# PSUM banks for short-lived results by a ledger of the plan, and an earlier read of the accumulated y

## The chip, the cores and the metric

The kernel runs on one core of one Trainium2 chip. The metric is the device time of one execution in microseconds; before the change it is 1008.92 us, the median of 3 runs (1008.82 to 1009.45). A core has engines that work side by side, each through its own queue in order: TensorE for matrix products (PE in the profile, its weight loads PEld), VectorE (DVE), ScalarE (ACT), GpSimd (POOL), and SyncE (SP), which here issues transfers. TensorE writes its products into PSUM, which has eight banks of 128 partitions x 512 fp32 values; the results of a bank must be read by VectorE or ScalarE before the bank can be written anew.

## The reference, cut to what matters

The input x is 8 sequences of 1024 tokens with 128 values each, all in fp32. Three layers follow one another:

```python
x = x + 0.5 * ffn(layernorm(x))
x = x + attention(layernorm(x))      # causal, one head of 128, rotary positions
x = x + 0.5 * ffn(layernorm(x))      # the same weights
```

`ffn` is a mixture of 16 experts of width 64. A sigmoid of `x @ gate_w.T` scores the experts; of the scores plus a bias the best four are chosen; their scores, divided by their sum and times 2.5, are the weights. Each expert computes `silu(x @ w1.T) * (x @ w3.T)`, then `@ w2.T`; a shared expert with the weight 1 is added. The kernel computes all 16 experts for every token, with the weight 0 for those not chosen.

## The kernel before

**Groups and periods.** The work of the two ffn layers is cut into 32 groups of 512 tokens (4 tiles of 128; 8 sequences x 2 groups x 2 layers). Each group has one period p, 0 to 31. The order is layer one of sequences 0 to 3, then alternately the second ffn layer of a sequence and the first of a later one, and at last the second of sequences 4 to 7. A period has two phases of eight steps. In the first, step k computes 128 hidden units (two experts) for 512 tokens: `gate(k)` (L265) and the product of `up(k)` (L278), on ScalarE the SiLU (L280), on VectorE the product of the two (L282), on GpSimd the weighting with the expert weights (`weigh`, L286). In the second phase, step k adds the product of those units with the down matrix to y (`down`, L291), which accumulates in one PSUM bank. `close` (L302) then adds y and the shared expert's result on VectorE into yT in SBUF; a period later `add` turns yT back (L324) and adds it to x (L327).

**Slots.** All else goes into slots between these steps: U0 to U8 around the first phase and D0 to D8 in the second; slot Uk+1 follows step k, and slot Dk follows `down(k)`, so that D8 stands alone at the end, after `close`. A plan written out by hand gives each piece its slot. Of the pieces, these matter here:

- `turn` of a group (L168): transposes of the normalised x, copied by ScalarE (L169). The routing: `route_a` (L193, copied by L198), `route_b` (L202), `score` (L207 on ScalarE), then `top_a`, `top_b`, `top_c` on VectorE (L211 to L239, the last writes comb), then `spread`: a transpose of comb (L248), a copy (L250) and the transfers that bring the weights to all partitions (cd, cb). In the steady part these have the slots D4, D5, D7, D7, D8, D8, U1 and U3.
- Attention: `Heads` project q, k and v of a sequence (L394, read by L398, L399 and L400; L408, copied by L412). A `Query` is one tile of 128 queries: `scores` (L427), mask, maximum, exponent (L438), two `turn`s (transposes L454, copied by ScalarE L458 or VectorE L460) and `attend` (L466), whose result VectorE adds to x in L470 and follows with the statistics L145 and L146. A tile i attends to i + 1 tiles, so its attend can be narrow (2 passes) or wide (16). A period starts two or three queries; their attends are in D7, in U2 of the next period and, with a third, in U5.
- `Shared`: the shared expert for a pair of groups, in U0 and U2 of even periods (L342, L346, L347, L356, L362).

The Tile framework puts in the waits between engines; nothing is reordered after that.

**PSUM banks.** Bank 0 takes the up product of even k, then y; bank 1 the gate of even k; 2 and 3 those of odd k. Queries use 4 and 5 or 2 and 3 for scores, projections and the shared expert use 5 and 4. All other results, those of `turn`, `route_a`, `route_b`, `spread`, `add`, `values` and `attend`, are short-lived: written by a few matmuls and read by one or two instructions. They ask `other_bank()` (L74), which goes round through a list of spare banks: 6 and 7, and bank 1 as well from D0 to D7. There are 353 such takes.

Of the kernel before, what the change touches and what calls it, by code (L numbers as in the profile page):

```python
# [26 lines left out]
def kernel(  # L27
# [24 lines left out]
    NP = EI // P  # L52
# [10 lines left out]
    dram = ctx.enter_context(tc.tile_pool(name="dram", bufs=3, space=bass.MemoryType.DRAM))  # L63
    ps_all = ctx.enter_context(tc.tile_pool(name="ps_all", bufs=1, space=PSUM))

    psum = ps_all.tile([P, 8 * W], F32, name="psum")

    def bank(i, n=1):
        return psum[:, i * W : (i + n) * W]


    spare = [6, 7]

    def other_bank():  # L74
        spare.append(spare.pop(0))
        return bank(spare[-1])

    def tiles_of(ap):
        return ap.rearrange("p (j q) -> p j q", q=P)
# [59 lines left out]
    def stats(key, b, tiles):  # L139

        if key not in mvs:
            mvs[key] = small.tile([P, NT, 2], F32, tag="mv", name=f"mv_{key}", bufs=16)
        for t in tiles:
            st = small.tile([P, 6], F32, tag="st", name=f"st_{key}_{t}")
            nc.vector.bn_stats(st, xs[b][:, t, :])  # L145
            nc.vector.bn_aggr(mvs[key][:, t, :], st)  # L146
# [18 lines left out]
    def transposed(key, g, xn, hT):  # L165
        pt = other_bank()
        for j in range(GT):
            nc.tensor.transpose(tiles_of(pt)[:, j, :], xn[:, j, :], ident)  # L168
        nc.scalar.copy(hT, pt)  # L169
# [3 lines left out]
    class Group:  # L173
# [15 lines left out]
        def route_a(self):  # L189

            lt = other_bank()[:, :P]
            for j in range(GT):
                nc.tensor.matmul(  # L193
                    lt[j * SW : (j + 1) * SW, :], gw, self.hT[:, j * P : (j + 1) * P],
                    start=True, stop=True, tile_position=(0, j * SW),
                )
            self.lt = small.tile([P, P], F32, tag="lt", name=f"lt_{self.nm}", bufs=2)
            nc.scalar.copy(self.lt, lt)  # L198

        def route_b(self):  # L200
            self.lg = other_bank()[:, :P]
            nc.tensor.transpose(self.lg, self.lt, ident)  # L202
# [279 lines left out]
    NPER = NG * len(order)  # L482
# [7 lines left out]
    def at(p, slot, *fs):  # L490
        jobs.setdefault((p, slot), []).extend(fs)
# [3 lines left out]
    def when(p, slot):  # L495
        return p * len(slots) + slots.index(slot)

    turn_of = {(gr.layer, gr.b, gr.g): p for p, gr in enumerate(groups)}


# [2 lines left out]
    for p in range(3, 29):  # L503
        for n in range(2 if p in (15, 21) or (p % 2 == 0 and p != 26) else 3):
            if not queue:
                continue
            b, i = queue.pop(0)
            starts.setdefault(b, p)
            q = Query(heads[b], i)
            s, first, e, t0, t1, a = (  # L510
                ((p, "U7"), 4, (p, "D0"), (p, "D3"), (p, "D5"), (p, "D7")),
                ((p, "D2"), 2, (p, "D5"), (p, "D8"), (p + 1, "U0"), (p + 1, "U2")),
                ((p, "D4"), 4, (p, "D7"), (p + 1, "U3"), (p + 1, "U4"), (p + 1, "U5")),
            )[n]
            at(*s, lambda q=q, first=first: q.scores(first))
            at(*e, q.exp)
            at(*t0, lambda q=q: q.turn(0))
            at(*t1, lambda q=q: q.turn(1))
            at(*a, q.attend)
            done[b, i] = when(*a)  # L520
# [4 lines left out]
    for b in range(B):  # L525
        h, st = heads[b], starts[b]
        ready = when(turn_of[0, b, 1] + 1, "U7")
        if b == 0:
            p0, p1 = st - 1, st - 1
            places = ("U8", "D0", "D2", "D3", "D5", "D6", "D7", "D8")  # L530
        else:
            p0, p1 = st - 2, st - 1
            places = ("D0", "D3", "D5", "D8", "U1", "U4", "U5", "U6")
        assert ready < when(p0, places[0])
        at(p0, places[0], h.deviations)
        at(p0, places[1], lambda h=h: h.norm(0))
        at(p0, places[2], lambda h=h: h.norm(1))
        at(p0, places[3], lambda h=h: h.turn(0))
        at(p1, places[4], lambda h=h: h.turn(1))
        at(p1, places[5], lambda h=h: h.project(0, 0))  # L540
        at(p1, places[6], lambda h=h: h.project(1, 0))
        at(p1, places[7], lambda h=h: h.values(0))
        at(st, "U4", lambda h=h: h.project(0, 1))
        at(st, "U5", lambda h=h: h.project(1, 1))
        at(st, "U6", lambda h=h: h.values(1))


    for p, gr in enumerate(groups):
        steps = (
            gr.norm_a, gr.norm_b, gr.turn, gr.route_a, gr.route_b, gr.score, gr.top_a, gr.top_b,  # L550
            gr.top_c, gr.spread,
        )
        if p == 1:
            steps = steps[1:]
            places = [(0, s) for s in ("U3", "U5", "U6", "U8", "D0", "D1", "D2", "D3", "D6")]
        else:
            places = [(p - 2, s) for s in ("U5", "D1", "D4", "D5", "D7", "D7", "D8", "D8")]
            places += [(p - 1, "U1"), (p - 1, "U3")]
        if p > 0:
            for f, place in zip(steps, places):  # L560
                at(*place, f)
        if gr.layer == 1:
            for t in range(gr.g * GT, (gr.g + 1) * GT):
                assert done[gr.b, t] < when(p - 2, "U5")

        if p % 2 == 0:
            pair = Shared(groups[p : p + 2])
            if p == 0:
                at(0, "D0", pair.up)
                at(0, "D3", pair.down)  # L570
            else:
                jobs[p, "U0"] = [pair.up] + jobs.get((p, "U0"), [])
                at(p, "U2", pair.down)

        at(p + 1, "U3", gr.add)
        if gr.layer == 0:
            t = gr.g * GT
            for s in ("U5", "U7"):
                at(p + 1, s, lambda b=gr.b, t=t: stats(f"a{b}", b, (t, t + 1)))
                t += 2  # L580


    for b in range(2, B):
        p = turn_of[0, b, 0]
# [11 lines left out]
        nc.sync.dma_start(out=cs, in_=rope)  # L596

    def run(p, slot):
        for f in jobs.pop((p, slot), []):
            f()  # L600

# [18 lines left out]
    for p, gr in enumerate(groups):  # L620
        run(p, "U0")
        for k in range(NP):
            gr.up(k)
            if p == 0 and k < 2:
                run(p, f"U{k + 1}")
                if k == 1:
                    gr.weigh(k)
            else:
                gr.weigh(k)
                run(p, f"U{k + 1}")  # L630
        for k in range(NP + 1):
            if k < NP:
                gr.down(k)
            else:
                gr.close()
            if k == 0:
                spare.insert(0, 1)
            elif k == NP:
                spare.remove(1)
            run(p, f"D{k}")  # L640
    for p in (NPER, NPER + 1):
        for slot in slots:
# [73 lines left out]
```

## Time and profile before

| | |
|---|---|
| median of 3 runs | 1008.92 us (1008.82 to 1009.45) |
| the profiled execution | 1008.44 us, span 1006.7 us |
| TensorE matmuls | 985.8 us busy, 98% of the span |
| VectorE / ScalarE / GpSimd | 67% / 44% / 45% busy |
| mean granted TensorE clock | 0.999 of full |
| L265, L278, L291, 512 passes of 128x512 each | 264.0, 262.3, 247.1 us |
| transfers | 80.26 MB, 80 GB/s |

The span is the time from the first to the last instruction of the program in one profiled execution; the time of that execution has something around it. A row of the profile names line, engine, operation, what is written <- what is read, the shape and the count; where it ends in brackets, the engine sat idle that long before it, and what follows the arrow ended the wait. An fp32 product is two passes of a weight load and a matmul each, a transpose one. Matmuls are pipelined: the next starts before the one before has its end in the profile.

### The profile page before, as it was taken

Reading aid. Unit: us, or ns where it says so; the run is one execution under the profiler, and the core shown is the slowest. Engines: PE = TensorE matmul, PEld = TensorE weight load, DVE = VectorE, ACT = ScalarE, POOL = GpSimd, SP = SyncE. Lnnn points to the kernel's source line nnn. Section 1 sums busy time; section 2 is a strip of 40 time slices with the busy share of each in tenths; the row PEclk is TensorE's granted clock in tenths of the full one; section 3 lists DMA queues with packets and bytes.
Section 4 is the critical chain, followed back from the end, with each engine's and each line's share of the span. In section 5 each row is a group of like instructions: output and inputs, shape, how many; then the busy total and the mean of one; then the engine's idle time right before and its main releaser. Section 6 shows DMA issues by size and latency. Waiting matters only on the chain.

```text
span 1006.7 us, 11656 instructions
## 1 busy us (share of the span) xinstructions
PE 985.8 (98%) x3654; PEld 515.9 (51%) x3654; DVE 670.5 (67%) x2035; ACT 444.2 (44%) x798; POOL 450.7 (45%) x379
## 2 busy tenths in 40 slices
PE   8999999999999999999999999999999999999998
PEld 5444455554555555455554555555555555455543
DVE  6776777668666676666768656776667756664553
ACT  3444535444544444343544444544444444443331
POOL 2455556154633464334625455234644454423444
PEclk9999999999999999999999999999999999999999
DMA  6654343043312542145303453034421333134440
GB/s 164 164 122 91 86 85 86 1 105 85 86 41 55 117 85 60 27 96 116 86 15 71 95 117 76 12 83 96 96 59 37 75 96 85 36 72 96 96 95 21
DMA packets 56910, 80.26 MB, mean 80 GB/s; under 512 B 3600, under 2 KB 23440, under 8 KB 56720
## 3 DMA queue, kind: packets, MB, share of 16 engines
q1 hardware_dynamic: 55568, 78.26, 34.5%
q10 hardware_dynamic: 1280, 1.26, 0.4%
q8 instruction: 28, 0.46, 0.2%
q14 instruction: 34, 0.28, 0.1%
HBM read 74.27 MB, written 5.24 MB: 79 GB/s over the span
## 4 chain that ended last, share of the span: by engine, by line
PE 91%; DVE 5%; ACT 1%; POOL 1%; DMA 1%; issue 1%; SPq 0%; DVEq 0%; POOLq 0%
PE psum L291 21%; PE psum L265 20%; PE psum L278 20%; PE psum L466 6%; PE psum L427 6%; PE psum L454 3%; PE psum L342 3%; PE psum L394 3%; PE psum L168 2%; PE psum L356 2%; PE psum L408 1%; PE psum L193 1%; PE psum L324 1%; DVE x L470 1%; DMA cb<-cd 1%
## 5 line engine op out<-in xcount | busy, mean ns | idle before, releaser
L286 POOL TENSOR_TENSOR hidT<-hidT,cb 128x512 f32<-128x512 f32 x256 | 323.2, 1270 | 516.3 <-DVE hidT L282 479.2
L265 PE MATMUL psum<-hT,wg 128*128 128x512 f32 x512 | 264.0, 597 | 0.9 <-DVE x L470 0.5
L278 PE MATMUL psum<-hT,wu 128*128 128x512 f32 x512 | 262.3, 594 | 1.2 <-DVE yT L302 1.2
L291 PE MATMUL psum<-hidT,wd 128*128 128x512 f32 x512 | 247.1, 599 | 0.0
L282 DVE TENSOR_TENSOR hidT<-psum,sg 128x512 f32<-128x512 f32 x256 | 175.4, 687 | 104.0 <-PE psum L278 97.7
L280 ACT ACTIVATE sg<-psum 128x512 f32<-128x512 f32 x256 | 152.4, 598 | 203.7 <-PE psum L265 191.8
L278 PEld LDWEIGHTS psum<-hT,wu 128*128 128x128 f32 x512 | 96.5, 190 | 126.1 <-issue 98.8
L291 PEld LDWEIGHTS psum<-hidT,wd 128*128 128x128 f32 x512 | 89.8, 190 | 80.4 <-issue 74.2
L265 PEld LDWEIGHTS psum<-hT,wg 128*128 128x128 f32 x512 | 88.4, 192 | 68.4 <-issue 61.4
L466 PEld LDWEIGHTS psum<-v,prT 128*128 128x128 f32 x576 | 74.4, 192 | 30.6 <-issue 28.7
L466 PE MATMUL psum<-v,prT 128*128 128x128 f32 x576 | 74.6, 275 | 0.0
L458 ACT COPY prT<-psum 128x512 f32<-128x512 f32 (+2 forms) x64 | 32.4, 506 | 93.9 <-PE psum L454 93.8
L427 PE MATMUL psum<-k,q 128*128 128x512 f32 (+2 forms) x192 | 72.4, 486 | 0.0
L159 DVE TENSOR_SCALAR xn_f<-x,mv_f,rs_f 128x128 f32<-128x128 f32 x128 | 68.5, 595 | 1.9 <-POOL rs_f L152 1.7
L470 DVE SCALAR_TENSOR_TENSOR x<-psum,rl,x 128x128 f32<-128x128 f32 x64 | 22.1, 346 | 69.4 <-PE psum L202 44.8
L427 PEld LDWEIGHTS psum<-k,q 128*128 128x128 f32 x192 | 36.5, 190 | 45.9 <-issue 44.7
L454 PEld LDWEIGHTS psum<-ident,pr 128*128 128x128 f32 x288 | 35.4, 141 | 39.6 <-issue 29.6
L454 PE MATMUL psum<-ident,pr 128*128 128x128 f32 x288 | 47.4, 276 | 5.7 <-DVE x L470 5.2
L433 DVE TENSOR_REDUCE top<-psum 128x1 f32<-128x128 f32 (+3 forms) x64 | 48.5, 758 | 2.2
L438 ACT ACTIVATE pr<-psum,top 128x128 f32<-128x128 f32 (+3 forms) x64 | 47.7, 746 | 0.3
L431 DVE TENSOR_TENSOR psum<-psum,causal 128x128 f32<-128x128 f32 x64 | 19.0, 297 | 41.3 <-PE psum L427 40.8
L152 POOL TENSOR_TENSOR rs_f<-rs_f,neg_half 128x4 f32<-128x4 f32 x32 | 32.4, 1013 | 16.8 <-DVE rs_f L151 16.3
(86 smaller groups left out, 1010.9 us busy)
## 6 DMA issues: line engine op xcount, KB each, us to landing
cb<-cd SPq DMA_DIRECT2D x124, 512.0 KB, 8.2
x<-in_x SPq DMA_DIRECT2D x16, 256.0 KB, 10.3
out_x<-x SPq DMA_DIRECT2D x15, 256.0 KB, 2.4
cb<-cd SPq DMA_DIRECT2D x8, 256.0 KB, 5.8
cd<-cT SPq DMA_DIRECT2D x32, 32.0 KB, 1.8
cs<-in_rope SPq DMA_DIRECT2D x1, 1024.0 KB, 9.7
wg<-in_w_gate ACTq DMA_DIRECT2D x2, 256.0 KB, 6.4
wu<-in_w_up ACTq DMA_DIRECT2D x2, 256.0 KB, 6.0
```

The lines of the kernel that those rows point to most:

```text
L159: nc.vector.tensor_scalar(xn[:, j, :], xs[b][:, t, :], mvs[key][:, t, 0:1], rstd[:, j : j + 1], ALU.subtract, ALU.mult,)
L265: nc.tensor.matmul(bank(2 * (k % 2) + 1), wg[:, units], self.hT, start=True, stop=True)
L278: nc.tensor.matmul(u_ps, wu[:, units], self.hT, start=True, stop=True)
L280: nc.scalar.activation(sg, g_ps, AF.Silu)
L282: nc.vector.tensor_tensor(hid, u_ps, sg, ALU.mult)
L286: nc.gpsimd.tensor_tensor(hid, hid, self.cb[:, k, :], ALU.mult)
L291: nc.tensor.matmul(self.y, wd[:, k, :], self.hidT[:, k, :], start=(k == 0), stop=(k == NP - 1))
L427: nc.tensor.matmul(s[:, c:e], h.q[:, i * P : width], h.k[:, c:e], start=True, stop=True)
L433: nc.vector.tensor_reduce(top, s[:, :width], AX.X, ALU.max)
L438: nc.scalar.activation(self.pr[:, : self.width], self.s[:, : self.width], AF.Exp, bias=self.top, scale=SCALE, accum_out=self.h.rl[:, self. ...
L454: nc.tensor.transpose(tp[:, j, :], self.pr[:, (k + j) * P : (k + j + 1) * P], ident)
L466: nc.tensor.matmul(o, self.prT[:, j, :], self.h.v[:, j, :], start=(j == 0), stop=(j == i))
```

## The change

`other_bank()` no longer goes round through a list. A table `held` notes for each bank the slots in which the plan uses it for something of its own (the calls of `hold`). A bank 1 to 5 is free in a slot if it is held neither in it nor in the one before or after; 6 and 7 are always free. Of the free ones, the bank whose last take is the oldest is given. The lists that put bank 1 in and out at D0 and D8 go away. The projections in `Heads` are put into the plan by a loop at the same slots as before; only the ledger is told of them. And `close` is called right behind `down(7)`, ahead of the pieces of slot D7, where it came after them before.

```diff
-    spare = [6, 7]
+    held = {n: set() for n in range(8)}
+    by_age = [6, 7, 1, 2, 3, 4, 5]
+    now = [-1]
 
     def other_bank():
-        spare.append(spare.pop(0))
-        return bank(spare[-1])
+        for n in by_age:
+            free = not held[n] & {now[0] - 1, now[0], now[0] + 1} and now[0] >= 0
+            if n > 5 or free:
+                by_age.remove(n)
+                by_age.append(n)
+                return bank(n)
...
+    def hold(banks, first, last):
+        for n in banks:
+            held[n] |= set(range(when(*first), when(*last) + 1))
+
+    for p in range(NPER):
+        hold((0,), (p, "U1"), (p, "D8"))
+        hold((1,), (p, "U1"), (p, "U8"))
+        hold((2, 3), (p, "U1"), (p, "D1"))
...
             at(*s, lambda q=q, first=first: q.scores(first))
+            hold((first, first + 1), s, e)
...
-        at(p1, places[5], lambda h=h: h.project(0, 0))
-        at(p1, places[6], lambda h=h: h.project(1, 0))
+        for w in range(2):
+            for p, slot, g in ((p1, places[5 + w], 0), (st, ("U4", "U5")[w], 1)):
+                at(p, slot, lambda h=h, w=w, g=g: h.project(w, g))
+                hold((5 - w,), (p, slot), (p, slot))
         at(p1, places[7], lambda h=h: h.values(0))
-        at(st, "U4", lambda h=h: h.project(0, 1))
-        at(st, "U5", lambda h=h: h.project(1, 1))
...
                 at(0, "D3", pair.down)
+                hold((4, 5), (0, "D0"), (0, "D4"))
...
                 at(p, "U2", pair.down)
+                hold((4, 5), (p, "U0"), (p, "U3"))
...
     def run(p, slot):
+        now[0] = when(p, slot)
...
             if k < NP:
                 gr.down(k)
-            else:
+            if k == NP - 1:
                 gr.close()
-            if k == 0:
-                spare.insert(0, 1)
-            elif k == NP:
-                spare.remove(1)
             run(p, f"D{k}")
```

## The prediction

> **What bounds the kernel now.** I read the busy shares first, then the chain that ended last, then the list of waits, and last the order of time around the waits on TensorE's path.
>
> ```profile
> PE 985.8 (98%) x3654; PEld 515.9 (51%) x3654; DVE 670.5 (67%) x2035; ACT 444.2 (44%) x798; POOL 450.7 (45%) x379
> ...
> PE 91%; DVE 5%; ACT 1%; POOL 1%; DMA 1%; issue 1%; SPq 0%; DVEq 0%; POOLq 0%
> ```
>
> TensorE sets the time: 91% of the chain. VectorE's 5% is what TensorE waits for, so the question is how many waits of TensorE the change takes away. The waits of TensorE's matmuls, as total, times, longest:
>
> ```profile
> PE psum L454 <- DVE x L470: 5.2, 13, 0.4
> PE psum L248 <- DVE comb L239: 2.0, 2, 1.4
> PE psum L248 <- ACT prT L458: 1.7, 7, 0.2
> PE psum L248 <- DVE x L470: 1.7, 3, 0.7
> ```
>
> The reported ends of matmuls overlap the next start, so idle time understates a wait. I take starts: a 128x512 pass starts 0.429 us after the one before it, a 128x128 pass 0.11. Whatever a start is later than that is lost. Over the trace this adds up to 40 us, 7 of them in the first 40 us. I sorted these gaps by what had ended some 0.05 us before the late start: the last writer of an input, or the last reader of the PSUM bank that is written. Two places carry most of it; rows in order of time show start, then duration.
>
> Slot D8 of period 9, one of 13 such places, where the bank of the attend in D7 comes round again:
>
> ```profile
> 317.79 0.27 PE L202 MATMUL psum<-ident,lt 128*128 128x128 f32 x1
> 318.06 0.35 DVE L470 SCALAR_TENSOR_TENSOR x<-psum,rl,x 128x128 f32<-128x128 f32 x1 [3.43 <-PE psum L202]
> ...
> 318.47 0.33 PE L454 MATMUL psum<-ident,pr 128*128 128x128 f32 x1 [0.40 <-DVE x L470]
> ```
>
> L454 starts 0.68 after L202 where 0.11 would do: 0.57 lost. Its own input, pr, was ready 5 us earlier. The second is U3 of period 13, at the end of a VectorE run without a pause that began at 418.15; TensorE's rows, then VectorE's:
>
> ```profile
> 424.30 0.60 PE L324 MATMUL psum<-ident,yT 128*128 128x128 f32 x4
> 425.61 0.30 PE L248 MATMUL psum<-ident,comb 128*64 128x128 f32 x1 [0.70 <-DVE x L470]
> ```
>
> ```profile
> 424.46 0.28 DVE L239 SCALAR_TENSOR_TENSOR comb<-sel,tot 128x64 f32<-128x64 f32 x1
> 424.61 0.68 DVE L282 TENSOR_TENSOR hidT<-psum,sg 128x512 f32<-128x512 f32 x1
> 425.21 0.34 DVE L470 SCALAR_TENSOR_TENSOR x<-psum,rl,x 128x128 f32<-128x128 f32 x1
> ```
>
> L248 waits for L470 only because of its bank: 0.87 from start to start beyond the step. Its input comb was done at 424.74, and that is the limit behind the bank.
>
> **What the Trainium skill says.** Perfetto Trace Analysis, section Matmuls, wants independent matmul groups to rotate through different banks so that the evacuation of one overlaps the next. The trace agrees as to the price of too few: 0.57 us in D8. The same page, section Per-engine timelines, says that TensorE's reported end is an estimate; 0.40 idle against 0.57 lost is why I count starts. Its section Identifying Dependency Chains says that an instruction that waits on several engines may get an EventSemaphore in front. The trace has 49 on TensorE's queue, nearly all of 0.051 us; at 39 of the 46 that stand between matmuls the next start is within 0.001 us of its step.
>
> **The change, part by part.** *The ledger* takes no instruction away and adds none; it renames banks. I went through all 353 takes in program order by its rule. Before, 295 use banks 6 and 7, and 58 bank 1. After, 180 use 6 and 7, 44 bank 1, 129 banks 2 to 5. For each I put the end of the old bank's last reader against the start of the first matmul, both from the trace. Before, one take in ten has less than 0.06 us between them; after, one in ten less than 1.65.
>
> (a) L454 in D8 of periods 5, 8, 9, 11, 12, 14, 15, 18, 19, 21, 22, 25, 28: its new bank was last read 4.2 us or more ahead, its input ready 3.4 us or more ahead. 13 x 0.562 = 7.3, and 13 x 0.055 = 0.7 for the slower step behind such a start (0.166 against 0.11). Sum 8.0.
> (b) L248 behind L470 in U3 of periods 7, 17, 21: 0.64 + 0.64 + 0.19 = 1.47, the new bank free for 9 us. Period 13: 0.87 becomes 0.06 (comb), 0.81. Sum 2.3.
> (c) L265 in U0 behind D7's L470 in bank 1, periods 7, 17, 21: 0.33 + 0.35 + 0.13 = 0.8.
> (d) L454 in U0 of 5, 15, 25 behind the copy L458 of D8: 0.30 + 0.40 + 0.30, and 3 x 0.055: 1.2.
> (e) L168 in D8 behind L207: five times 0.039 and the slower step, 0.5.
>
> *What stays.* In U3 of even periods banks 1 to 5 are all held, and three takes share 6 and 7 as before: L248 behind L458, 11 times, 3.5 us.
>
> *What it adds.* A take in D8 may get bank 1, which the first gate (L265) of the next period writes right behind U0. In D8 of period 26 this is close:
>
> ```profile
> 866.45 0.37 ACT L458 COPY prT<-psum 128x256 f32<-128x256 f32 x1
> ...
> 866.60 0.70 PE L265 MATMUL psum<-hT,wg 128*128 128x512 f32 x1 [0.18 <-DVE x L470]
> ```
>
> L265 would start at 866.89, 0.29 later. With the wait for L302 behind it gone 0.13 of that is left, and the 0.74 that L324 waits for L470 in U3, with its slow step 0.8, is won: net 0.7. Other periods with bank 1 in D8 have 1.04 us or more of room. In D8 of period 2, L408 gets bank 5, which L400 reads until 90.75, 0.27 past its old start: 0.33, swallowed as told below. EventSemaphores in front of matmuls that now wait on more engines cost between 0 and 0.051 each; I take 0, as the 39 show.
>
> *y out of PSUM earlier.* One L302 (0.66 us; the next instruction starts 0.57 to 0.6 after it) per period goes ahead of D7's L470, L145 and L146. It issues no DMA and passes nothing on SP's or POOL's queue. Behind it VectorE holds D7's L470. With a wide attend in D7 VectorE is idle there (3.43 us before the L470 of 318.06): L302 is free, and the run that follows is 0.57 shorter. With a narrow one, as in period 6, the last product ends near 220.0, and L470 slips from 220.32 to about 220.65. No matmul writes its bank in the microsecond after that, and the run still ends 0.27 earlier. Without the idle time L302 would gain nothing for those behind it, as period 3 shows below. It ends L278's waits for L302 in U0 of 7, 17, 21, 13, 31: 3 x 0.16 + 2 x 0.09 = 0.66, and eight slow steps around them (0.533 against 0.429), 0.8.
>
> *Where nothing is won.* Period 3 has the longest wait for L302. VectorE's rows, then TensorE's:
>
> ```profile
> 92.26 0.67 DVE L400 TENSOR_TENSOR k<-psum,cs 128x512 f32<-128x512 f32 x1
> 92.85 0.68 DVE L302 TENSOR_TENSOR yT<-psum,ys 128x512 f32<-128x512 f32 x1
> ```
>
> ```profile
> 93.59 1.12 PE L278 MATMUL psum<-hT,wu 128*128 128x512 f32 x2 [1.19 <-DVE yT L302]
> ...
> 99.52 0.30 PE L248 MATMUL psum<-ident,comb 128*64 128x128 f32 x1 [0.64 <-DVE comb L239]
> ```
>
> VectorE has no pause from 90.05 to 99.46. L302 only changes places with this L400, so comb comes when it came, and L248 with it: waits of 1.36 and 0.19 give 0. The 0.47 in U0 of period 1 (L265 behind L207) gives 0 too: the store of cd that began at 37.98, before that wait, leads through the load of cb and POOL to the L168 of 58.21.
>
> **The sum.** 8.0 + 2.3 + 0.8 + 1.2 + 0.5 + 0.7 + 0.66 + 0.8 = 15.0 us. I take 1.0 off for what becomes late next: with TensorE 0.6 us earlier, the attends of U2 come close to waiting for L460, which has 0.39 to 0.59 us of room in eight of the periods behind (a); the shorter VectorE run gives back 0.57 only with wide attends. The profiled execution took 1008.44 (span 1006.7, 1.7 around it): 994.4. The median shown is 1008.92, 0.5 above it: 994.9.
>
> **The rivals.** *VectorE's run is the bound* (998): if the run from D7's L470 to U3's comb gets no shorter (L302 starts late, or instructions beside it grow), (a) keeps only the room of L460 in periods 6, 9, 12, 16, 19, 23, 26, 29, 3.3 of 5.0, and U3 of 7, 13 and 17 only the 0.8 up to comb, 1.8 less: 15.0 - 1.7 - 1.8 - 0.5 = 11.0. For it: VectorE without a pause in those stretches. Against: the 3.43 us idle just ahead.
> *More is won* (990.5): the 3.5 us in U3 of even periods too. The ledger has no bank free there.
> *It doesn't do what it says* (1008): takes that wait get a young bank again, and only L302's 0.66 is won. Bank 6 or 7 does come in several D8 slots, but was last read four slots earlier.
> *Slower* (1011 and above): last readers are now on changing engines, and takes get an EventSemaphore whose 0.051 us is exposed. With one for each of 353 takes, 18 us against 15, it ends 3 above; it decides from 15 / 0.051 = 294 on. The 39 without a cost speak against it.
>
> **How the numbers follow.** The sum 0.69, VectorE's run 0.19, more won 0.05, no effect 0.03, slower 0.04. A measurement of this kernel can tell 0.2%, 2 us, from no change. Faster 0.93, same 0.03, slower 0.04. The range 992.3 to 999.5 holds the first two cases: downwards the sum without the 1.0 and 1.6 for slow steps missed, upwards 1.5 past the rival.
>
> **What would show it.** Right: L454 in D8 starts 0.11 after L202; L302 starts with the end of the last product and ahead of L470; L248 in odd periods starts behind comb; its 11 waits for L458 remain; L265 of period 27 waits for L458; period 3 gains nothing. Wrong: new waits of L466 for L460 or of L248 for comb, or more EventSemaphores on TensorE's queue with late starts behind them.

## The result and the profile after

The changed kernel takes 995.16 us (median of 4 runs, 994.21 to 996.32) against 1009.18 us before (4 runs, 1008.82 to 1009.93): ratio 0.9861, 95% interval 0.9844 to 0.9878, 14.0 us less. The forecast was 994.9. The profiled execution took 994.21 us, its span is 992.3.

All lines from `other_bank` to the plan are 6 further down in this kernel: L454 before is L460, L470 is L476, L302 is L308, L248 is L254, L265 is L271, L278 is L284. The page's busy shares and its chain:

```profile
PE 979.5 (99%) x3654; PEld 516.8 (52%) x3654; DVE 671.5 (68%) x2035; ACT 442.2 (45%) x798; POOL 450.5 (45%) x379
...
PE 93%; DVE 3%; ACT 1%; DMA 1%; issue 0%; POOL 0%; SPq 0%; POOLq 0%; DVEq 0%
```

The instructions are the same in number and VectorE is as busy as before; its share of the chain falls from 5% to 3%. So nothing was computed faster; TensorE waits less. Its waits (total, times, longest), which answer to those shown of before:

```profile
PE psum L254 <- DVE comb L245: 2.0, 2, 1.4
PE psum L254 <- ACT prT L464: 1.7, 7, 0.2
...
PE psum L271 <- ACT prT L464: 0.5, 1, 0.5
```

The transposes of the probabilities (L460) are gone from this list, and L254 no longer waits for L476. The two kinds of wait that were to stay are there, and the one that was to come (L271). Slot D8 of period 9, TensorE's rows:

```profile
314.86 0.27 PE L208 MATMUL psum<-ident,lt 128*128 128x128 f32 x1
314.97 0.27 PE L460 MATMUL psum<-ident,pr 128*128 128x128 f32 x1
```

and VectorE's beside it:

```profile
313.28 0.69 DVE L308 TENSOR_TENSOR yT<-psum,ys 128x512 f32<-128x512 f32 x1 [1.58 <-PE psum L297]
315.06 0.35 DVE L476 SCALAR_TENSOR_TENSOR x<-psum,rl,x 128x128 f32<-128x128 f32 x1 [1.09 <-PE psum L472]
```

L460 starts 0.11 us after L208 where it started 0.68 after it, and before L476, which frees the bank of the attend, has even begun. L308 has moved into the idle time ahead of L476. In the median period it started 1.81 us after the end of the last product down; now it starts 0.04 after it.

U3 of period 13, TensorE and then VectorE:

```profile
419.20 0.60 PE L330 MATMUL psum<-ident,yT 128*128 128x128 f32 x4
419.85 0.30 PE L254 MATMUL psum<-ident,comb 128*64 128x128 f32 x1
```

```profile
419.52 0.27 DVE L245 SCALAR_TENSOR_TENSOR comb<-sel,tot 128x64 f32<-128x64 f32 x1
```

L254 now starts 0.06 after comb is done (419.79), 0.21 later than its step, where 0.87 was lost to the bank. The input is the limit behind the bank, as the forecast had it.

To compare kernels I count what starts show. For each two matmuls in a row I take the distance of their starts less the step of the first one's shape (0.429 us for 512 columns, 0.322 for 384, 0.215 for 256, 0.111 for 128; starts inside a group of four of L193 or of eight of L356 are left out, and the step behind the last start of such a group is 0.203 or 0.306), and add up all that is over 0.03:

| kernel | median us | span of its profile | lost between starts | span less lost |
|---|---|---|---|---|
| before | 1009.18 | 1006.7 | 40.0 | 966.7 |
| the change | 995.16 | 992.3 | 25.8 | 966.5 |
| ledger alone | 997.4 | 995.1 | 28.7 | 966.4 |
| early close alone | 1007.52 | 1005.3 | 38.7 | 966.6 |
| D8 as before | 1002.98 | 1000.6 | 34.0 | 966.6 |
| banks 6, 7, 2, 3 | 999.29 | 997.7 | 31.1 | 966.6 |
| banks 6, 7, 1 | 1004.64 | 1003.1 | 36.4 | 966.7 |
| 4 and 5 released | 992.08 | 989.9 | 23.6 | 966.2 |
| and bank 1 from U0 | 990.47 | 988.5 | 22.3 | 966.2 |
| and spread later | 989.84 | 986.8 | 20.6 | 966.2 |

The last column is the same to 0.5 us in all ten. All ten kernels have the same 3654 matmuls of the same shapes, so this column could differ only by a changed step or by what lies before the first and behind the last matmul; neither changed. What the change is worth is the sum of TensorE's lost starts.

### The profile page after: what moved, and what is told of

Its sections match the earlier page's. It is cut to its first block, busy times and chain, and to the rows that moved or that the text cites. A ratio compares the mean times of both kernels' runs of the same rounds, so it can differ in the third digit from the quotient of the medians.

```text
span 992.3 us, 11654 instructions
## 1 busy us (share of the span) xinstructions
PE 979.5 (99%) x3654; PEld 516.8 (52%) x3654; DVE 671.5 (68%) x2035; ACT 442.2 (45%) x798; POOL 450.5 (45%) x379
## 4 chain that ended last, share of the span: by engine, by line
PE 93%; DVE 3%; ACT 1%; DMA 1%; issue 0%; POOL 0%; SPq 0%; POOLq 0%; DVEq 0%
PE psum L297 22%; PE psum L271 21%; PE psum L284 21%; PE psum L472 6%; PE psum L433 6%; PE psum L460 3%; PE psum L348 3%; PE psum L400 3%; PE psum L174 2%; PE psum L362 2%; PE psum L414 1%; PE psum L199 1%; PE psum L330 1%; DMA cb<-cd 1%; PE psum L254 1%; PE psum L141 1%
## 5 line engine op out<-in xcount | busy, mean ns | idle before, releaser
L271 PE MATMUL psum<-hT,wg 128*128 128x512 f32 x512 | 263.7, 597 | 0.5 <-ACT prT L464 0.5
L284 PE MATMUL psum<-hT,wu 128*128 128x512 f32 x512 | 261.9, 593 | 0.6 <-DVE hidT L288 0.5
L288 DVE TENSOR_TENSOR hidT<-psum,sg 128x512 f32<-128x512 f32 x256 | 175.4, 687 | 104.1 <-PE psum L284 95.9
L284 PEld LDWEIGHTS psum<-hT,wu 128*128 128x128 f32 x512 | 96.9, 190 | 124.1 <-issue 95.7
L271 PEld LDWEIGHTS psum<-hT,wg 128*128 128x128 f32 x512 | 88.1, 191 | 67.3 <-issue 58.3
L472 PEld LDWEIGHTS psum<-v,prT 128*128 128x128 f32 x576 | 74.4, 192 | 30.6 <-issue 28.5
L472 PE MATMUL psum<-v,prT 128*128 128x128 f32 x576 | 74.6, 275 | 0.0
L308 DVE TENSOR_TENSOR yT<-psum,ys 128x512 f32<-128x512 f32 (+1 forms) x33 | 22.1, 673 | 58.0 <-PE psum L297 57.6
L460 PEld LDWEIGHTS psum<-ident,pr 128*128 128x128 f32 x288 | 36.0, 141 | 30.0 <-issue 29.6
L460 PE MATMUL psum<-ident,pr 128*128 128x128 f32 x288 | 46.5, 273 | 0.0
L175 ACT COPY hT<-psum 128x512 f32<-128x512 f32 x32 | 18.7, 585 | 47.7 <-PE psum L174 47.7
```

The lines of the kernel that those rows point to most:

```text
L271: nc.tensor.matmul(bank(2 * (k % 2) + 1), wg[:, units], self.hT, start=True, stop=True)
L284: nc.tensor.matmul(u_ps, wu[:, units], self.hT, start=True, stop=True)
L288: nc.vector.tensor_tensor(hid, u_ps, sg, ALU.mult)
L460: nc.tensor.transpose(tp[:, j, :], self.pr[:, (k + j) * P : (k + j + 1) * P], ident)
L472: nc.tensor.matmul(o, self.prT[:, j, :], self.h.v[:, j, :], start=(j == 0), stop=(j == i))
```

## Experiments

The theory: each late start is worth what its bank costs; the early L302 takes its own waits away and shortens VectorE's run so that no data wait comes in place of those for banks. Rival A: L302's place is worth only its own waits. Rival B: VectorE's run from D7 to U3 is the bound, and banks alone win little. Ratios are to the kernel before as it ran beside each kernel: 1008.97 us (25 runs) for the ledger alone, the early close alone, D8 as before and the release of banks 4 and 5, 1009.27 us (8 runs) for the others.

**The ledger alone**

```diff
-            if k == NP - 1:
+            if k == NP:
                 gr.close()
```

> The change with close back behind the pieces of D7 (the ledger alone). Theory (each wait is worth what its bank costs, and the early L302 shortens VectorE's run so that no data wait takes its place): L278's waits for L302 in U0 and the slow steps around them come back, 1.5 us; TensorE, 0.6 us earlier in U2, now waits for L460 in eight periods, 1.7 us by the room they had before (0.39 to 0.59), and a little more for comb in U3 of 7, 13, 17: 998.4 us. Rival A (L302's place is worth only its own waits): 996.7. Rival B (VectorE's run is the bound, so banks alone win little): 1003 or more.

Measured: 997.4 us (997.0 to 999.12), ratio to before 0.989 (0.9875 to 0.9905). Rival B falls: banks alone win 11.6 us. The runs reach from just above rival A's number past that of the theory, so the time does not choose between these two; the trace shows that neither had the mechanism right. The waits of which the theory spoke, those for the copy that is L460 in the kernel before, are not there. Instead the waits for L302 (here L308) have grown:

```profile
PE psum L284 <- DVE yT L308: 2.2, 5, 0.8
PE psum L254 <- DVE comb L245: 2.1, 2, 1.4
PE psum L254 <- ACT prT L464: 1.7, 7, 0.2
```

From start to start, L284 in U0 loses 0.54 us in periods 7 and 17, 0.65 in 13 and 0.32 in 21, where in the kernel before it lost 0.16, 0.16, 0.09 and 0.16. Before, TensorE waited for another bank just ahead of it: in periods 7, 17 and 21 the gate for its own, in period 13 L454 in D8 (0.57). With that wait gone TensorE stands in front of y sooner and waits there. With them L284 loses 3.4 us behind the first 40 us of the trace, against 1.1 with the whole change, and 0.7 more goes in slow steps. Having waited, TensorE then waits 0.65 us less for comb in U3 of 7, 13 and 17; in U3 of 10 and 20 L330 loses 0.43 and 0.44 behind L476, whose run is longer again.

**The early close alone**

```diff
-            else:
+            if k == NP - 1:
                 gr.close()
             if k == 0:
                 spare.insert(0, 1)
```

> The kernel before with close right behind the last product down, the spare list as it was. Theory: the 13 waits of D8 stay, since a wide attend's L470 comes no earlier; L302's waits go (0.7), the waits for the L470 of U2 in odd periods shrink by 0.57 or 0.27 (1.5), but with a narrow attend L470 of D7 comes 0.33 later and L265 of 7, 17, 21, 27 waits for it in bank 1 (1.3 lost): 1 to 2 us faster than before, about 1007.5. Rival B (VectorE's run is the bound): 5 us or more faster, 1004 or below.

Measured: 1007.52 us (21 runs, 1006.97 to 1008.98), ratio 0.9987 (0.998 to 0.9993), 1.5 us less. That is the theory's number, though its terms were larger (1.5 won in U3 and 1.3 lost at bank 1, where the trace has 0.95 and 0.9), and rival B falls again: VectorE's run is shorter here and the time hardly moves. Its waits and the U0 of period 7 show both halves of the account; this is the waits view, with the line numbers of before:

```profile
PE psum L454 <- DVE x L470: 5.2, 13, 0.4
...
PE psum L265 <- DVE x L470: 1.5, 3, 0.5
```

and VectorE, then TensorE, in order of time:

```profile
220.13 0.69 DVE L302 TENSOR_TENSOR yT<-psum,ys 128x512 f32<-128x512 f32 x1 [4.38 <-PE psum L291]
220.74 0.34 DVE L470 SCALAR_TENSOR_TENSOR x<-psum,rl,x 128x128 f32<-128x128 f32 x1
```

```profile
220.26 0.38 PE L454 MATMUL psum<-ident,pr 128*128 128x128 f32 x2
221.13 1.13 PE L265 MATMUL psum<-hT,wg 128*128 128x512 f32 x2 [0.49 <-DVE x L470]
```

The 13 waits of D8 are untouched. With this narrow attend L302 goes first and L470 comes later, and L265 still needs its bank: this wait grew, from 1.3 to 2.3 us over all L265 in U0. L278 lost 0.9 us less, the slow steps 0.5 less and U3 0.95 less. Alone, the early close pays at one bank most of what it wins at another.

Alone the parts win 11.6 and 1.5 us, together 14.0. The late starts of the traces put what comes on top at 1.6 us rather than 1.0. Each part removes a wait that the other brings when it stands alone: the early close those for y that the ledger uncovers (L284, 2.3 us more than with both), the ledger the growth of L265's wait for bank 1 (0.9). The waits for comb, which are shorter with the ledger alone, take some of this back.

**D8 as before, all else changed**

The first take in D8 of the 13 periods gets the bank of the attend in D7 again:

```diff
+    again = {p * 2 * (NP + 1) + 2 * NP + 1 for p in (5, 8, 9, 11, 12, 14, 15, 18, 19, 21, 22, 25, 28)}
+    last_attend = [6]
...
+        if now[0] in again:
+            again.remove(now[0])
+            n = last_attend[0]
```

> The change, but the first take in D8 of the 13 periods that waited there before gets the bank of D7's attend again. Theory: each wait of 0.56 and the slow step behind it come back in full, 13 x 0.62 = 8.0 us over the change: 1003.2. Rival B (TensorE would have waited for VectorE a little later anyway): part of it is absorbed, 5 us or less over the change: 1000 or below.

Measured: 1002.98 us (1002.57 to 1004.09), ratio 0.9941 (0.9929 to 0.9954), 7.8 us above the change. In its trace the starts of L454 lose 7.1 us in 13 places again, and the slow steps behind them 0.7. The waits view (L454 is L475 here, L470 is L491):

```profile
PE psum L475 <- DVE x L491: 5.0, 13, 0.4
PE psum L269 <- DVE comb L260: 2.0, 2, 1.4
```

So 8 of the 14 us are this one bank in D8, and nothing later would have taken them back. It is also what a plain sum of the late starts gives.

**Which banks: 6, 7, 2 and 3, or 6, 7 and 1**

```diff
-    by_age = [6, 7, 1, 2, 3, 4, 5]
+    by_age = [6, 7, 2, 3]
```

> The change with only banks 6, 7, 2 and 3 in the ledger's list. These are free in D7 and D8 and not in U2 and U3. Theory, from the rows of the changed kernel's trace and the banks this list gives: D8 stays without waits; back come L248 behind the L470 of U2 in four odd periods (3.0 us), L454 of U0 behind the copy L458 of D8 (1.2), L324 behind L470 (0.45), less the waits for comb that they cover: 4 to 5 us over the change, 999.6. Rival (more banks help everywhere alike): four of seven banks keep about half of the 14 us, 1002.

Measured: 999.29 us (999.06 to 1000.37), ratio 0.9905 (0.9889 to 0.9921), 4.1 us above the change. The waits of D8 stay away, those of U3 come back, and L460 (L454 before) of U0 waits for the copy of D8 again (1.2 us, as forecast):

```profile
PE psum L254 <- DVE x L476: 2.7, 3, 0.9
PE psum L254 <- DVE comb L245: 2.0, 2, 1.4
PE psum L254 <- ACT prT L464: 1.7, 7, 0.2
```

```diff
-    by_age = [6, 7, 1, 2, 3, 4, 5]
+    by_age = [6, 7, 1]
```

> The change with only banks 6, 7 and 1 in the ledger's list: the banks that the kernel before had, but bank 1 in D8 as well and from D1 only. Theory, from the rows of the changed kernel's trace: D8 itself is mostly free of waits, but the bank that D8 takes is wanted at once: L265 in U0 behind the readers of D8 (6.9 us in 14 periods), L454 and L168 in U0 and D8 (1.4), L248 and L324 in U3 behind L470 (3.5), some 12 us in sum if none covers another, 10 if some do: 1005 to 1007. Rival (taking by age is what helps, whatever the banks): 1000 or below.

Measured: 1004.64 us (1003.72 to 1005.51), ratio 0.9955 (0.9942 to 0.9968), 9.5 us above the change, just under the range of the theory and well above the rival's. L271 in U0 loses 6.5 us against 0.6, with 1.35 more in slow steps:

```profile
PE psum L271 <- ACT hT_a L175: 1.8, 3, 0.7
...
PE psum L271 <- DVE x L476: 1.5, 3, 0.5
...
PE psum L271 <- ACT prT L464: 0.7, 3, 0.4
```

Of the 3.5 us in U3 only 0.8 came: having waited in U0, TensorE meets a VectorE that has caught up. In period 7 L254 loses 0.31 behind the 0.66 that L271 lost, where with banks 2 and 3 it loses 1.07 and L271 nothing. So taking by age is not enough by itself: with these banks the change wins 4.6 of its 14 us, the early read of y included. Two banks that are free when D8 and what follows want them are worth more than one that is wanted right behind it. The two lists also differ in length, four banks and three, and no run takes from the same seven banks by another rule than age; what each of the two adds is not shown.

**Releasing banks 4 and 5**

```diff
-                hold((4, 5), (p, "U0"), (p, "U3"))
+                hold((4, 5), (p, "U0"), (p, "U1"))
```

> The change, with banks 4 and 5 held for the shared expert in even periods only from U0 to U1 in place of U3, so that the takes of U3 may have them (their reader L362 in the kernel before ends 1.5 us ahead of L248 in period 10). Theory: the 11 waits of L248 for the copy L458, 3.8 us in the changed kernel's trace, go; comb was ready 1.5 us or more ahead in all of them, so nothing takes their place: 991.4. Rival: the wait moves to the copies L362 or into U4 and U5, where 4 and 5 are wanted for the projections: 994 to 996.

Measured: 992.08 us (991.05 to 992.71), ratio 0.983 (0.9817 to 0.9844), 3.1 us below the change. All 11 waits for the copy are gone, 3.76 us of lost starts. A new one came in place, L271 in U0 of period 15 behind the copy of a transposed xn in D8, 0.67 us and a slow step: the ages moved, and D8 of period 14 now gets bank 1 for it.

```profile
PE psum L271 <- ACT hT_a L175: 0.5, 1, 0.5
...
PE psum L271 <- ACT prT L464: 0.5, 1, 0.5
```

**Bank 1 not in D8**

```diff
-        hold((1,), (p, "U1"), (p, "U8"))
+        hold((1,), (p, "U0"), (p, "U8"))
```

> The kernel with banks 4 and 5 released after U1, and bank 1 held from U0 in place of U1, so that no take of D8 gets it. In the profile with 4 and 5 released, L265 in U0 of period 15 starts 0.67 late behind the copy L169 of D8 and that of period 27 0.62 late behind the copy L458, each with a slow step of 0.1. Theory: both go and nothing takes their place, since 2 to 5 are free in D8: 1.4 us less, 990.7. Rival: the takes move to banks 2 and 3 and the gate of step 1 waits for them: no gain, 992.

Measured: 990.47 us (990.24 to 991.67), ratio 0.9819 (0.9806 to 0.9833). Both waits of L271 are gone from its trace and, behind the first 60 us, none has come. The median is 1.6 us below that with 4 and 5 released, and 4.7 below the change. The runs of the first pair overlap a little; behind the first 60 us the trace loses 1.5 us less, where 1.4 was forecast.

**spread one slot later**

```diff
-            places += [(p - 1, "U1"), (p - 1, "U3")]
+            places += [(p - 1, "U1"), (p - 1, "U4")]
```

> As the run with bank 1 held from U0, and spread moved from U3 to U4, one step of 0.86 us later. Left in U3 are the waits of L248 for comb: 0.8 in period 3 and 0.2 to 0.25 in 7, 13 and 17. Theory (the end of VectorE's run is only felt where TensorE asks for comb): they go, 1.2 to 1.5 us less, 989.4; the transfers of cb come 0.86 later and are wanted some 15 us later only. Rival A: VectorE's run is felt at the next place (products L282 and their bank), and less than 0.5 is won, 990.5. Rival B: the later transfer collides with another one and delays the weighting, slower.

Measured: 989.84 us (988.96 to 990.84), ratio 0.9809 (0.9796 to 0.9823). Against the kernel before it the medians differ by 0.6 us and the runs overlap, so the times alone don't tell the two apart. Behind the first 60 us the trace loses 0.9 us less. All waits for comb but the one at the start are gone; in period 3, rival A has its part, since the end of VectorE's run is now felt at the bank of a product (L288 is L282 of before):

```profile
98.81 1.02 PE L271 MATMUL psum<-hT,wg 128*128 128x512 f32 x2
100.17 0.70 PE L284 MATMUL psum<-hT,wu 128*128 128x512 f32 x1 [0.33 <-DVE hidT L288]
```

0.5 of the 0.8 us of this period came back one product later. Rival B, a late transfer, does not show: no wait for cb is among TensorE's or in the time.

The last three kernels are faster than both the kernel before and the change.

## Why the prediction was right

**The method.** Starts, not idle time, was the right measure. The sum of late starts fell by 14.2 us and the span by 14.3. What was not to change, the span without the lost starts, moved by 0.2. One number beside the sum is off: with the banks of the changed program and the times of the trace before, one take in ten has less than 2.2 us, not 1.65; no term of the sum uses it.

**(a), D8.** Forecast 8.0, found 8.0: all 13 late starts (7.31) and the slow steps behind them (0.7). Undone alone it cost 7.8.

**(b), U3 of odd periods.** Forecast 2.3, found 1.6. This is the term that was mis-sized. Periods 7 and 17 kept 0.24 and 0.25, period 13 0.21, all behind comb; the forecast left 0.06 in 13 and nothing in the others. I had let TensorE win the waits of U0, the slow steps around them and U3 one by one, though all of them together may not exceed the room up to comb, plus what VectorE's run becomes shorter. I had that room, 0.8, in the rivals and left it out of this term.

**(c), (d), (e)** and the waits of L278 in 7, 13, 17 and 21: every one of these late starts is gone, as forecast. The 0.09 in period 31 stayed, with the slow step behind it 0.2: nothing stood ahead of L302 in period 30, where it started 0.04 us behind the last product before the change as well.

**The new waits.** L265 of period 27 (L271 now) waits for the copy, as shown by the waits view: it loses 0.62 from start to start against 0.35, forecast 0.29 more, found 0.28. In D8 of period 2 the new wait is 0.32, forecast 0.33, and swallowed: TensorE's rows of period 3 after the change,

```profile
92.94 1.12 PE L284 MATMUL psum<-hT,wu 128*128 128x512 f32 x2 [0.16 <-DVE yT L308]
...
99.48 0.30 PE L254 MATMUL psum<-ident,comb 128*64 128x128 f32 x1 [0.64 <-DVE comb L245]
```

L254 starts at 99.48 against 99.52: the wait for y shrank from 1.36 to 0.32 us, but D8 lost 0.4 with its slow step and L284 two steps later 0.64 behind a product (L288) where it had lost 0.19. Period 3 won nothing, because VectorE's run ends when it ended. In period 1, too, the 0.47 went into a later wait, which grew from 0.38 to 0.95.

**What stays.** L248 behind L458 in even periods, 3.5 us: found 3.8. In periods 4 and 24 this wait grew from 0.16 and 0.17 to 0.29 each, since L324 just ahead of it no longer waits.

**The early y.** L302 starts 0.04 us behind the last product in 28 of the 31 periods that are not the last; the narrow attends did push L470 back, and no matmul waited for it. That it was needed for the whole gain was forecast for another reason than the one found: not the copy L460 in U2, where TensorE lost nothing even with the ledger alone, but y in U0.

**The 1.0 taken off.** The waits that it stood for, of the attends for the copy L460 (line numbers of before), did not come. The room of 0.39 to 0.59 us had been counted to the first pass of the attend, but the first pass that reads what L460 writes is the ninth, 0.89 us later. The ledger alone shows it, in U2 of period 9 (L460 is L466 here, the attend L472):

```profile
287.06 0.55 DVE L466 COPY prT<-psum 128x384 f32<-128x384 f32 x1
287.56 1.73 PE L472 MATMUL psum<-v,prT 128*128 128x128 f32 x14
```

The attend starts 0.05 us before the copy has ended and none of its passes is late; in all eight periods it starts 0.04 to 0.18 before that end. So the 1.0 was right by luck, by its size only, because (b) was 0.7 too large. The sum without it and with the (b) that was found is 14.3, the fall of the span.

**The rivals.** VectorE's run as the bound (998): with the whole change L302 did move into the idle time, and 14.0 us were won where this rival had 11.0. The ledger alone leaves L302 where it was and wins 11.6, near the rival's number, but not by its account: D8 keeps its whole gain, no attend waits for that copy, and TensorE waits for y in U0 rather than for comb in U3 of 7, 13 and 17. EventSemaphores on TensorE's queue are 57 after the change where they were 49, and the lost starts have no room for a price. More was to be won, though not by this ledger: it took a shorter hold on 4 and 5, which the forecast had taken as given.

## What to carry to other kernels

Where one engine is full, list its late starts from start to start and sort them by what ended last, an input or a reader of the buffer. Give the late buffer another that was last read long ago, then go on to the input behind it: what the starts up to there lose together can't be won beyond its room. A table of when a buffer is held is only as good as its ends: a hold two slots too long cost 3.1 us here, and one that began a slot too late at bank 1 then cost about 1.5.

## What the runs showed beyond that

- A matmul start that had to wait costs more than its wait: the next step behind it was 0.054 to 0.104 us longer (0.166 in place of 0.11 for 128 columns, 0.533 in place of 0.429 for 512). Over the 13 places of D8 that is 0.7 us. Behind the late starts of L248 it was only 0.026. A wait is not the only thing that brings such a step: in the kernel before, 0.533 also stands behind all 32 uses of L193 and all 16 of L356, where no wait shows.
- Two waits in a row on one engine hide each other. When the gate's wait for bank 1 went away, the wait for y behind it rose from 0.16 to 0.54 us; a list of waits does not show what stands behind each of them.
- The first 60 us differ between these ten profiles by up to 0.9 us (7.6 to 8.6 lost between starts), which is more than some of the effects above. Each kernel has one profile, so how much of this is chance is not shown.
